# An LSTM with a mixture of experts behind it: which products fill the gaps between the recurrent steps, in which order, and how the last group of steps ends

## The chip, the cores and the metric

The kernel runs on one core of a Trainium2 chip. The metric is the device time of one execution in microseconds; the number given for a kernel is the median of its runs. An execution taken by the hardware profiler gives the trace; its span runs from the program's first to its last instruction.

## The reference

Two sequences (N = 2) of 1024 steps with 256 features go through an LSTM with 256 hidden units. Then every token goes through a router over eight experts, of which the two best count, and through two shared experts. Both layers add to their input.

```python
def step(carry, xw_t):
    prev_h, prev_c = carry
    a = xw_t + prev_h @ Wh
    i, f, o = sigmoid(a[:, :256]), sigmoid(a[:, 256:512]), sigmoid(a[:, 512:768])
    g = tanh(a[:, 768:])
    next_c = f * prev_c + i * g
    next_h = o * tanh(next_c)
    return (next_h, next_c), next_h
x = x + hs                                  # hs: all next_h
shared = sum_e (silu(x @ s_w1[e].T) * (x @ s_w3[e].T)) @ s_w2[e].T / 2
gates = top-2 of sigmoid([x, cond] @ W_router.T), normalized
routed = sum_e gates[:, e] * (gelu(x @ r_w1[e].T) @ r_w2[e].T)
x = x + (shared + routed) / 4
```

The code above is shortened: the reference writes the gates, the sums and the reshapes out. All is float32.

## The kernel before, in words

One Python loop over `t` (L728) writes out all 1024 LSTM steps; each step needs the h of the step before, so the steps run one after the other. A step has these parts:

- **The recurrent block** (L746 to L756): 32 products of h with parts of `wh_sb`, each on 32 weight columns of the array. The four quarters `q` of the output lie on four groups of 32 partitions. In the profile every product is two passes[...], so the block is 64 MATMUL records.
- **The gap**: what TensorE is given between this block and the next one (L757 to L779). It is described below.
- **The cell**: VectorE transposes the gates in PSUM (L787), ScalarE takes sigmoid and tanh (L790, L791), VectorE and ScalarE compute the cell and its tanh (L794 to L807), and VectorE writes the new h (L810) in two halves. The next recurrent block waits for it.

Everything else is spread over the steps by a small planner, the class `Fill`. Four queues hold closures with a cost each: for TensorE (`pe`), for ScalarE, and two for VectorE. The router and experts of a finished group of tokens are put into these queues by `experts` (L286); the products of the LSTM's inputs with Wx (`queue_inputs`, L631) go into the same TensorE queue. `GROUPS` (L36) says how many steps make a group, `PACES` (L38) by how many steps later its products shall be issued, and `run_pe` (L117) takes in each step so many products from the queue that it empties in time, within a cost of `ROOM` = 4 and as long as one of two PSUM banks is free for those that open one. All products go through one helper, so the profile shows them at L255; they are told apart by their tiles: `ps<-wh_sb,h` is the recurrent block, `ps_f<-...` are products of experts, router and LSTM inputs, `ps<-ident,inputs` puts the LSTM's input terms into the PSUM bank where the gates of eight later steps are summed ("input product" from here on), and `ps<-ident` is a product of the identity with itself whose result nobody reads ("idle product").

The gates of eight steps share one pair of PSUM tiles (`TH` = 8). So at each eighth step (an opening, `t % TH == 0`) the tiles change, and during eight steps the eight input products for the next tiles are issued, mostly one in a step. In the gap of a step the order before is: expert products (L758), or, if there were none in this step and none at the opening, an idle product of 256 columns (L761 to L765), and then the input products (L767 to L779).

How many input products a step gets also depends on a count of TensorE's instructions: `fill.issued` counts 4 for a product, and `WAITS` lists the steps in which the program has a further instruction that only waits. Instructions are fetched in blocks of `FETCH` = 256. The loop at L772 chooses the smallest number of input products that keeps the next block's border out of the next `EARLY` = 16 instructions; if none does, the last input product is cut into pieces (`pieces` of `inject`, L654) so that the border falls within them.

Behind the loop, the last group (32 steps, 64 tokens) is issued without steps between (`drain`, L851). What is left of the group before it stands ahead of it in the queue. `last_add` (L532) adds an expert's result to the sum `acc`; 64 tokens lie on two halves of the partitions, with four experts on each. After the last expert a product with `fold` adds the two halves, ScalarE copies the result, and one DMA stores it.

Of the kernel before, what the change touches and what calls it, by code (L numbers as in the profile page):

```python
# [9 lines left out]
F32 = mybir.dt.float32  # L10
# [11 lines left out]
Q = 4  # L22
# [10 lines left out]
TOP_K = 2  # L33
LAST = 32

GROUPS = [128] * 3 + [32] + [128] * 4 + [64, LAST]  # L36

PACES = [128] * 7 + [56, 31, 0]  # L38
FILL_BANKS = 2


# [5 lines left out]


FETCH = 256
EARLY = 16  # L50
WAITS = (
    1, 8, 16, 24, 32, 40, 48, 56, 64, 72, 80, 88, 96, 104, 112, 120, 128, 136, 144, 149,
    152, 157, 160, 160, 165, 168, 176, 181, 184, 189, 192, 197, 200, 208, 216, 224, 232,
    240, 248, 256, 264, 272, 280, 288, 296, 304, 312, 320, 328, 336, 344, 352, 360, 368,
    376, 384, 392, 400, 408, 416, 419, 421, 423, 424, 428, 430, 432, 435, 437, 439, 440,
    440, 447, 448, 456, 464, 472, 480, 488, 496, 504, 512, 520, 528, 529, 536, 544, 552,
    560, 568, 576, 584, 592, 600, 608, 616, 624, 632, 640, 648, 656, 664, 672, 680, 688,
    688, 696, 704, 712, 720, 728, 736, 744, 752, 760, 768, 776, 784, 792, 800, 808, 816,
    824, 832, 840, 848, 856, 864, 872, 880, 888, 896, 904, 912, 920, 928, 930, 933, 935,
    936, 940, 942, 944, 947, 949, 951, 952, 956, 958, 960, 963, 965, 968, 976, 984, 992,  # L60
    999, 1000, 1004, 1006, 1008, 1011, 1013,
)
ISSUED = -188
OUT_SCALE = 1.0 / (NS + TOP_K)
# [9 lines left out]
class Fill:  # L74
# [36 lines left out]
    def run(self, queue, budget):  # L111
        while queue and queue[0][0] <= self.step and queue[0][1] <= budget:
            _, cost, fn = queue.popleft()
            budget -= cost
            fn()

    def run_pe(self, count, room):  # L117
        done = 0
# [16 lines left out]
def lstm_moe_kernel(  # L135
# [117 lines left out]
    def product(*operands, **how):  # L253
        fill.issued += 4
        nc.tensor.matmul(*operands, **how)  # L255
# [30 lines left out]
    def experts(t0, S):  # L286
# [215 lines left out]
        def last_shared_down(c):  # L502
            if c < 0:
                st["down"] = bank()
                x_kqj = st["down"][:W, 0, :].rearrange("p (q k j) -> p k q j", q=Q, k=K)
                for k in range(K):
                    product(
                        x_kqj[:, k], mov[k], ident_s,
                        start=(k == 0), stop=False, skip_group_check=True,
                    )  # L510
                return
            ps, n = st["down"], NS * HS // P
            for g in range(2):
                product(
                    ps[g * W : (g + 1) * W, 0, :], st["h_s"][:, c + g, :W], w2_sb[:, c + g, :],
                    start=(c + g == 1), stop=(c + 2 == n), skip_group_check=True,
                )
            if c + 2 == n:
                fill.to_dve(0.45, lambda: begin_sum(0, ps), lag=0)
# [11 lines left out]

        def last_add(e2, ps):  # L532
            acc = st["acc", 0]
            nc.vector.scalar_tensor_tensor(  # L534
                acc, ps[:, 0, :], st["gates"][:, e2 : e2 + 1], acc, ALU.mult, ALU.add
            )
            fill.let_go()
            if e2 == E // 2 - 1:
                both = bank()[:W, 0, :]
                product(both, fold, acc, start=True, stop=True)  # L540
                total = work.tile([P, D], F32, name="y")[:W]
                nc.scalar.activation(total, both, AF.Copy)  # L542
                nc.sync.dma_start(out=out_tn[t0 : t0 + S], in_=total)

        ups = [
            (int(j == 0), W // P if W > P else 1, lambda b=b, j=j: up(b, j))
# [181 lines left out]
    for t in range(T):  # L728
        fill.step = t
        grp, u = divmod(t, TB)  # L730
        if t % TH == 0:
            cur, nxt = nxt, [gates_tile(m) for m in range(K)]
            ps, turned, busy = [a[0] for a in cur], [a[1] for a in cur], nxt[0][2]
            spare = False
        if u == 0:
            sgm, gf = nxt_results
        if t == 1:
            queue_inputs(0, ROWS)
        if t == XB // 2:
            queue_inputs(1)  # L740
            due = XB
        if t == T - 1:
            residual(grp, int(t - TB in ends), TB)


        for k, m, pair in BLOCKS:  # L746
            for q in range(Q):
                w0 = q * D + m * P + pair * 64
                product(
                    ps[m][q * ROWS : (q + 1) * ROWS],  # L750
                    h_window(t, k, pair),
                    wh_sb[:, k, w0 : w0 + 64],
                    start=False,
                    stop=(t % TH == TH - 1 and k == K - 1 and pair == 1),
                    skip_group_check=True,
                )  # L756
        left = max(1, due - t)  # L757
        done = fill.run_pe(-(-len(fill.pe) // left), ROOM)  # L758
        if t % TH == 0:
            spare = not done  # L760
        if spare and not done:  # L761
            product(
                busy, ident, ident.unsqueeze(1).to_broadcast([P, 2, P]),
                start=(t % TH == 0), stop=False, skip_group_check=True,
            )  # L765

        if t // TH + 1 < T // TH:  # L767
            put = put if t % TH else 0
            fill.issued += WAITS.count(t)

            left = K * Q - put
            count = next(  # L772
                (n for n in range(max(0, t % TH + 1 - put), left + 1)
                 if -(fill.issued + 4 * n) % FETCH > EARLY), left)
            first = -(fill.issued + 4 * count) % FETCH
            for i in range(count):
                more = i == count - 1 and first <= EARLY
                inject(nxt, t // TH + 1, put, 2 + first // 4 if more else 1)
                put += 1  # L779

        rows = slice(N * (t % TH), N * (t % TH + 1))
        gates = [turned[m].rearrange("p (a r) -> p a r", r=PAIR)[:, :, rows] for m in range(K)]
        c_new = [cells[m][:, t % 2] for m in range(K)]
        seen = [stepp.tile([P, N], F32, name=f"seen{m}") for m in range(K)]

        def transpose(m):
            nc.vector.transpose(turned[m], ps[m])  # L787

        def squash(m):
            nc.scalar.activation(sgm[:, u, m, :, :, 1], gates[m][:, 0:3], AF.Sigmoid)  # L790
            nc.scalar.activation(gf[:, u, m, :, 0], gates[m][:, 3], AF.Tanh)  # L791

        def forget(m):
            nc.vector.tensor_mul(gf[:, u, m, :, 1], sgm[:, u, m, 2, :, 1], c_prev[m][:, :, 1])  # L794

        def cell(m):

            nc.vector.tensor_copy(seen[m], gf[:, u, m, :, 0])  # L798
            nc.vector.tensor_tensor_scan(  # L799
                c_new[m].rearrange("p n z -> p (n z)"),  # L800
                sgm[:, u, m, 0].rearrange("p n z -> p (n z)"),
                gf[:, u, m].rearrange("p n z -> p (n z)"),
                0.0, ALU.mult, ALU.add,
            )

        def squash_cell(m):
            nc.scalar.activation(cells[m][:, 2, :, 0], c_new[m][:, :, 1], AF.Tanh)  # L807

        def output(m):
            nc.vector.tensor_mul(h_cols(t + 1)[:, m], sgm[:, u, m, 1, :, 1], cells[m][:, 2, :, 0])  # L810

        for fn in (transpose, squash):
            for m in range(K):
                fn(m)
        for m in range(K):
            forget(m)
            cell(m)
            squash_cell(m)
        for m in range(K):
            output(m)  # L820
        if u == TB // 2 and t + TB < T:
            nxt_results = results()
        else:
            fill.run(fill.act, 1.0)
        c_prev = c_new
        if rest and t % LOAD == 0:
            load_next()
        if t == 2 * TB:
            lg = bank()[:, 0, :E]
            fill.banks -= 1  # L830
            fill.pe.extend((0, 1, lambda k=k: condition_scores(lg, k)) for k in range(K))
        if (t + 1) % XB == 0 and t + 1 + XB < T:
            queue_inputs((t + 1) // XB + 1)
        if u < TB - 1:
            fill.run_dve(0.6)
            continue
        if t < T - 1:
            residual(grp, int(grp == 0 or t - TB in ends), TB)
        if t in ends:
            residual(grp + 1, 0, 1)  # L840
            if t == T - 1:
                drain(fill)
                fill.last = True
                fill.banks += 4
            t0, S, pace = ends[t]
            experts(t0, S)
            due = t + pace
# [80 lines left out]
```

## Time and profile before

| what | value |
|---|---|
| median of three runs | 2257.78 us (2252.64 to 2258.61) |
| profiled execution, its own time | 2256.97 us |
| its span | 2254.8 us |
| mean granted TensorE clock | 0.996 |
| TensorE busy | 2033.5 us |
| VectorE busy | 1571.3 us |
| ScalarE busy | 909.5 us |
| time between the ends of the recurrent chain: first and last write of h (L810, second half) | 11.6 and 2233.9 us |
| last store issued (L543) | 2251.8 us |

The profile gives each instruction's start and length. An engine's busy time counts its own instructions; the idle time before an instruction is put down to the instruction whose semaphore ended it. A group's mean mixes shapes unless it says so. "PEclk" and the clock in the view by windows are the share of its full clock that TensorE was granted.

### The profile page before, as it was taken

The page shows a single profiled execution, that of the slowest core. Times are in us where ns is not written, and L with a number is a line of the kernel's source. Part 1 is how long each engine was busy: PE and PEld are TensorE (multiplying, and loading weights), DVE is VectorE, ACT ScalarE, POOL GpSimd, SP SyncE. Part 2 cuts the span into 40 slices and gives each one's busy share as a digit, 9 for nine tenths or more (in the row PEclk, how much of TensorE's full clock was granted, in tenths as well). Part 3 has the DMA queues.
Part 4 walks back from the last instruction along what each step waited for, and adds up shares of the span by engine and source line. Part 5 has one row for each costly group of instructions (what it writes and reads, how often), then busy time and mean ns, then how long its engine had stood idle before and what let it go on. Part 6 is the DMA issues. An engine that isn't in the chain of part 4 may idle for free.

```text
span 2254.8 us, 159246 instructions
## 1 busy us (share of the span) xinstructions
PE 2033.5 (90%) x70612; PEld 1484.8 (66%) x70612; DVE 1571.3 (70%) x11041; ACT 909.5 (40%) x6487; POOL 2.7 (0%) x9
## 2 busy tenths in 40 slices
PE   8988899888989889998798899988898988989998
PEld 6666666666666666777666666666666666667787
DVE  5666667776777667777667767676676776667776
ACT  3334344433444334443344443444434344334443
POOL 0000000000000000000000000000000000000000
PEclk9999999999999999999999999999999999999999
DMA  2111100000000000000000000000000000000000
GB/s 65 35 35 35 35 28 5 5 5 7 7 5 5 5 7 7 5 7 7 5 6 5 5 5 7 7 4 5 5 7 7 4 5 5 7 7 5 5 9 7
DMA packets 15330, 23.84 MB, mean 11 GB/s; under 512 B 2864, under 2 KB 14128, under 8 KB 14640
## 3 DMA queue, kind: packets, MB, share of 16 engines
q1 hardware_dynamic: 14352, 12.62, 1.9%
q8 instruction: 552, 9.04, 1.7%
q14 instruction: 138, 1.13, 0.2%
q10 hardware_dynamic: 288, 1.05, 0.1%
HBM read 11.56 MB, written 2.10 MB: 6 GB/s over the span
## 4 chain that ended last, share of the span: by engine, by line
PE 61%; DVE 36%; issue 3%; DMA 0%; SPq 0%; ACT 0%
PE ps L255 53%; DVE ps L787 10%; DVE c L799 10%; PE ps_f L255 8%; DVE results L794 7%; DVE seen L798 6%; DVE h L810 3%; DMA wh_sb<-in_wh_dram 0%; SPq L165 0%; DVE acc L534 0%; SPq L173 0%; SPq L171 0%; SPq L170 0%; DVE acc L492 0%; ACT y L542 0%
## 5 line engine op out<-in xcount | busy, mean ns | idle before, releaser
L255 PE MATMUL ps<-wh_sb,h 128*32 128x64 f32 x65536 | 1143.8, 221 | 214.3 <-DVE h L810 210.5
L255 PEld LDWEIGHTS ps<-wh_sb,h 128*32 128x32 f32 x65536 | 975.1, 110 | 393.1 <-DVE h L810 386.8
L787 DVE STREAM_TRANSPOSE ps<-ps 128x64 f32<-128x64 f32 x2048 | 543.4, 265 | 498.5 <-PE ps L255 426.0
L790 ACT ACTIVATE results<-ps 128x6 f32<-128x6 f32 x2048 | 361.3, 176 | 1103.8 <-DVE ps L787 1009.4
L810 DVE TENSOR_TENSOR h<-results,c 128x2 f32<-128x2 f32 x2048 | 314.2, 153 | 168.4 <-ACT c L807 168.2
L807 ACT ACTIVATE c<-c 128x2 f32<-128x2 f32 x2048 | 321.5, 157 | 217.5 <-DVE c L799 181.7
L799 DVE TENSOR_TENSOR_SCAN c<-results 128x4 f32<-128x4 f32 x2048 | 358.2, 175 | 0.0
L791 ACT ACTIVATE results<-ps 128x2 f32<-128x2 f32 x2048 | 342.4, 167 | 0.0
L798 DVE COPY seen<-results 128x2 f32<-128x2 f32 x2048 | 332.8, 162 | 0.0
L794 DVE TENSOR_TENSOR results<-results,c 128x2 f32<-128x2 f32 x2048 | 319.3, 156 | 0.0
L255 PEld LDWEIGHTS ps<-ident,inputs 128*32 128x32 f32 x2090 | 124.0, 108 | 265.7 <-issue 228.4
L255 PE MATMUL ps<-ident,inputs 128*32 128x64 f32 (+2 forms) x2090 | 263.9, 230 | 0.3
L255 PE MATMUL ps_f<-x2T,w_sb 128*128 128x256 f32 (+3 forms) x640 | 173.4, 379 | 0.0
L255 PE MATMUL ps_f<-x2T,r_sb 128*128 128x256 f32 (+3 forms) x640 | 173.2, 378 | 0.0
L255 PE MATMUL ps_f<-r_sb,h_r 128*128 128x256 f32 (+1 forms) x520 | 165.9, 419 | 0.9 <-DVE acc L492 0.9
L255 PEld LDWEIGHTS ps_f<-x2T,r_sb 128*128 128x128 f32 (+1 forms) x640 | 88.5, 184 | 22.8
L255 PEld LDWEIGHTS ps_f<-x2T,w_sb 128*128 128x128 f32 (+1 forms) x640 | 86.7, 184 | 21.8 <-issue 0.2
L255 PEld LDWEIGHTS ps_f<-r_sb,h_r 128*128 128x128 f32 (+1 forms) x520 | 80.0, 184 | 23.3 <-DVE acc L492 1.3
L255 PE MATMUL ps_f<-xT_sb,wx_sb 128*128 128x256 f32 (+2 forms) x384 | 84.5, 346 | 0.3 <-ACT inputs L613 0.3
L255 PE MATMUL ps<-ident 128*128 128x256 f32 x232 | 82.8, 443 | 1.4 <-POOL ident masks.py:199 1.4
L255 PE MATMUL ps_f<-w_sb,h_s 128*128 128x256 f32 (+1 forms) x256 | 82.6, 419 | 0.0
L492 DVE SCALAR_TENSOR_TENSOR acc<-ps_f,gate,acc 128x256 f32<-128x256 f32 (+1 forms) x128 | 61.1, 478 | 1.2 <-PE ps_f L255 1.0
(87 smaller groups left out, 475.1 us busy)
## 6 DMA issues: line engine op xcount, KB each, us to landing
r_sb<-in_r_w1T_dram SPq DMA_DIRECT2D x16, 128.0 KB, 2.5
r_sb<-in_r_w2T_dram SPq DMA_DIRECT2D x16, 128.0 KB, 2.1
out_dram<-acc SPq DMA_DIRECT2D x15, 128.0 KB, 2.1
xT_sb<-in_xT_dram SPq DMA_DIRECT2D x14, 128.0 KB, 2.5
wx_sb<-in_wx_dram ACTq DMA_DIRECT2D x2, 512.0 KB, 4.3
wh_sb<-in_wh_dram SPq DMA_DIRECT2D x2, 512.0 KB, 6.2
w_sb<-in_s_w1T_dram SPq DMA_DIRECT2D x8, 128.0 KB, 2.2
w_sb<-in_s_w3T_dram SPq DMA_DIRECT2D x8, 128.0 KB, 2.2
```

The costliest lines, as they stand in the source:

```text
L255: nc.tensor.matmul(*operands, **how)
L492: nc.vector.scalar_tensor_tensor(acc, ps, st["gate"][:, i, e : e + 1], acc, ALU.mult, ALU.add)
L787: nc.vector.transpose(turned[m], ps[m])
L790: nc.scalar.activation(sgm[:, u, m, :, :, 1], gates[m][:, 0:3], AF.Sigmoid)
L791: nc.scalar.activation(gf[:, u, m, :, 0], gates[m][:, 3], AF.Tanh)
L794: nc.vector.tensor_mul(gf[:, u, m, :, 1], sgm[:, u, m, 2, :, 1], c_prev[m][:, :, 1])
L798: nc.vector.tensor_copy(seen[m], gf[:, u, m, :, 0])
L799: nc.vector.tensor_tensor_scan(c_new[m].rearrange("p n z -> p (n z)"), sgm[:, u, m, 0].rearrange("p n z -> p (n z)"), gf[:, u, m].rearrang ...
L807: nc.scalar.activation(cells[m][:, 2, :, 0], c_new[m][:, :, 1], AF.Tanh)
L810: nc.vector.tensor_mul(h_cols(t + 1)[:, m], sgm[:, u, m, 1, :, 1], cells[m][:, 2, :, 0])
```

## The change

- **A wide product in each step.** Where a step has no expert product, an idle product of 256 columns is issued, whatever the opening had. For that, each opening must start the idle product's PSUM area: with 256 columns if the opening has no expert product, else with a product of 32 columns (`wide`), which stands first in the gap, with the wait for the PSUM tile's last reader.
- **Order in the gap.** A new method `ready_pe` counts, without issuing, how many expert products the step will take. Then the input products are issued, then the expert products, then an idle product if there was none of them and the step is no opening. At an opening the idle product comes first. The count of input products now looks for a border that is over `EARLY` = 12 instructions (20 in the last 32 steps) behind the end of the gap and not among its last two.
- **Groups.** The groups and paces at the end change, so that the group before the last is fully issued within the loop.
- **The last shared product** writes its two parts (`k`) on two halves of the partitions.
- **The last sum** is made in two halves of 128 columns: an addition, a product with `fold`, a copy and a DMA for each.

`WAITS` is rewritten for the new order (left out here).

```diff
-GROUPS = [128] * 3 + [32] + [128] * 4 + [64, LAST]
+GROUPS = [128] * 3 + [32] + [128] * 3 + [64] * 3 + [LAST]
-PACES = [128] * 7 + [56, 31, 0]
+PACES = [128] * 6 + [60, 60, 48, 27, 0]
-EARLY = 16
+EARLY = 12
...
+    def ready_pe(self, count, room):
+        done, banks = 0, self.banks
+        for opens, cost, _ in self.pe:
+            if done == count or opens > banks or cost > room:
+                break
+            banks -= opens
+            room -= cost
+            done += 1
+        return done
...
     def last_shared_down(c):
-                x_kqj = st["down"][:W, 0, :].rearrange("p (q k j) -> p k q j", q=Q, k=K)
+                x_kqj = st["down"][:, 0, :].rearrange("p (q k j) -> p k q j", q=Q, k=K)
                 for k in range(K):
                     product(
-                        x_kqj[:, k], mov[k], ident_s,
-                        start=(k == 0), stop=False, skip_group_check=True,
+                        x_kqj[k * W : (k + 1) * W, k], mov[k], ident_s,
+                        start=True, stop=False, skip_group_check=True,
                     )
...
     def last_add(e2, ps):
+            if e2 < E // 2 - 1:
+                cols = [slice(0, D)]
+            else:
+                cols = [slice(0, P), slice(P, D)]
+                total = work.tile([P, D], F32, name="y")[:W]
+            for i, c in enumerate(cols):
+                nc.vector.scalar_tensor_tensor(
+                    acc[:, c], ps[:, 0, c], st["gates"][:, e2 : e2 + 1], acc[:, c],
+                    ALU.mult, ALU.add,
+                )
+                if len(cols) > 1:
+                    both = bank()[:W, 0, :P]
+                    product(both, fold, acc[:, c], start=True, stop=True)
+                    nc.scalar.activation(total[:, c], both, AF.Copy)
+                    nc.sync.dma_start(out=out_tn[t0 : t0 + S][:, :, c], in_=total[:, c])
...
-        done = fill.run_pe(-(-len(fill.pe) // left), ROOM)
-        if t % TH == 0:
-            spare = not done
-        if spare and not done:
+        count = -(-len(fill.pe) // left)
+        done = fill.ready_pe(count, ROOM)
+        opens = t % TH == 0
+        if opens:
+            wide = busy[:, :1, :ROWS] if done else busy
             product(
-                busy, ident, ident.unsqueeze(1).to_broadcast([P, 2, P]),
-                start=(t % TH == 0), stop=False, skip_group_check=True,
-            )
+                wide, ident, ident[:, : wide.shape[2]].unsqueeze(1).to_broadcast(wide.shape),
+                start=True, stop=False, skip_group_check=True,
+            )
+            put = 0
+        then = 4 * (done or not opens) + WAITS.count(t)
+        early = EARLY + (8 if t >= T - LAST else 0)
         if t // TH + 1 < T // TH:
...
+            ways = range(max(0, t % TH + 1 - put), K * Q - put + 1)
+            first = [-(fill.issued + 4 * n + then) % FETCH for n in ways]
+            n = next((n for n, f in zip(ways, first) if early < f < FETCH - 2), ways[-1])
+            for i in range(n):
+                more = i == n - 1 and not early < first[-1] < FETCH - 2 and n == ways[-1]
+                inject(nxt, t // TH + 1, put, 2 + min(first[-1], early) // 4 if more else 1)
                 put += 1
+        fill.issued += WAITS.count(t)
+        fill.run_pe(count, ROOM)
+        if not (done or opens):
+            product(
+                busy, ident, ident.unsqueeze(1).to_broadcast(busy.shape),
+                start=False, stop=False, skip_group_check=True,
+            )
```

## The prediction

> **What bounds the kernel now.** I read the page first.
>
> ```profile
> span 2254.8 us, 159246 instructions
> ...
> PE 2033.5 (90%) x70612; PEld 1484.8 (66%) x70612; DVE 1571.3 (70%) x11041; ACT 909.5 (40%) x6487; POOL 2.7 (0%) x9
> ...
> PE 61%; DVE 36%; issue 3%; DMA 0%; SPq 0%; ACT 0%
> ```
>
> The chain of waits is TensorE and VectorE in turn: one serial loop of 1024 LSTM steps. No engine's busy share matters, only the length of a step. I took the period of all steps from the second L810 row of each: the median is 2.154 us, and 1023 periods sum to 2222.3. So 1023 x 2.154 = 2203.5 cannot move, and 18.7 us is excess that sits in single steps. Ahead of the loop lie 11.6 us (to the first h), behind the last h 20.9.
>
> The TensorE timeline (start, duration, engine, line, operation; in brackets the idle time before it and its releaser) shows what can lengthen a step: the gap between two recurrent blocks (64 passes on 32 weight columns; every product has two passes).
>
> ```profile
> 1017.37 1.13 PE L255 MATMUL ps_f<-r_sb,h_r 128*128 128x256 f32 x4
> 1018.49 1.10 PE L255 MATMUL ps<-wh_sb,h 128*32 128x64 f32 x64
> 1019.52 1.13 PE L255 MATMUL ps_f<-r_sb,h_r 128*128 128x256 f32 x4
> 1020.59 0.24 PE L255 MATMUL ps<-ident,inputs 128*32 128x64 f32 x1
> ```
>
> ```profile
> 1468.94 0.61 PE L255 MATMUL ps_f<-wr_sb,x2T 128*128 128x8 f32 x4
> 1469.49 0.30 PE L255 MATMUL ps<-ident,inputs 128*32 128x64 f32 x2
> ```
>
> Two expert products of 256 columns fill the gap: they begin 0.149 us behind the last recurrent pass, and the next 32-column pass begins 1.07 us after they did. The single records give these constants (medians over all steps): 32-column work to 128-column work 0.149; first to second pass of a 256-column product 0.320, every further pass 0.216; last 256-column pass to the next 32-column pass 0.309 (0.205 for 64 columns, 0.186 for 8); two passes of an input product 0.080 apart behind a 128-column product, but 0.049 + 0.056 = 0.105 where it comes straight behind the recurrent block. From the last recurrent pass to the next block, which waits for h, are 1.272 us. Two expert products need 0.149 + 0.320 + 0.432 + 0.309 = 1.210, so 0.06 is spare; one needs 0.778.
>
> Summing these constants over each gap of the built program (in its own order) gives 5.3 us of excess for the kernel before; its steps, without those of the next two causes, measure 5.2.
>
> Second cause, the clock, from the view by windows (the column after the busy times is the granted clock):
>
> ```profile
> 40.10:50.30 10.20, 8.07 (x252) 6.77 (x245) 4.26 (x34) 2.37 (x18) 0.00 (x0) 0.50 0.08 20
> ...
> 1470.30:1473.60 3.30, 3.30 (x100) 3.11 (x92) 1.39 (x11) 0.79 (x6) 0.00 (x0) 0.50 0.02 5
> 1750.20:1753.50 3.30, 3.30 (x82) 2.48 (x85) 1.59 (x12) 0.79 (x6) 0.00 (x0) 0.50 0.00 0
> ```
>
> The first hits steps 13 to 16, whose gaps are nearly empty (3.26 us over the median), the others the steps of router products of 8 columns (1.08 and 1.14). Together 5.5.
>
> Third cause, instruction fetch.
>
> ```profile
> q8 instruction: 552, 9.04, 1.7%
> ```
>
> ```profile
> 471.89 1.37 PE L255 MATMUL ps<-wh_sb,h 128*32 128x64 f32 x64 [0.42 <-DVE h L810]
> ```
>
> The program has 141,399 TensorE instructions, 256 for each of the 552 packets. Where a multiple of 256 falls on the last four products of a recurrent block, it often takes longer, as the 1.37 here against 1.10; elsewhere there is no cost. By position (28, 29, 30, 31 of 32) I count 27, 16, 46 and 2 such places, costing 0.02, 0.04, 0.13 and 0.4 us in the mean: about 8.0. 5.2 + 5.5 + 8.0 is the 18.7.
>
> **The change, part by part.**
>
> Input products ahead of the experts'. For one input product and two expert products the gap now needs 0.105 + 1.210 = 1.315, which is 0.043 over 1.272. Before it cost 0.024 to 0.037 in such steps. With the further steps of three or more products, gaps other than the openings below go from 5.3 to 7.3: +2.0. Gaps with one expert product stay under 1.272: nothing.
>
> A wide product in each step. Steps without an expert product get 256 columns, 0.778 + 0.105: hidden by the wait for h, which has 0.39 to spare. But each eighth step that has expert products gets a product of 32 columns first, then the input product, then the experts'. That is two more changes between 32 and 128 weight columns. No row has 32 columns. By the 8-column row the narrow product costs 0.133 + 0.186, by the 64-column row 0.160 + 0.205; I take 0.320, since 32 columns stream within the weight load (0.19) that bounds the 8-column row. It cannot be below nothing: it stands in program order ahead of the rest. Gap: 0.149 + 0.320 + 0.080 + 0.149 = 0.698, then one expert product 0.629 makes 1.327 (+0.055), two make 1.759 (+0.487). The built program has 18 such openings with two 256-column products (8.7 us, one without an input product), 68 with one (4.1), 20 with other mixes (2.8): +15.6. What is queued behind the narrow product's wait on ScalarE are these experts' products and the recurrent block; the same wait of 18 openings before was over at once (0.154 to the first pass). The same sum over a gap of four router products and one of 256 columns at step 928 gave 0.508 against 0.514 measured, so a full gap does push h out one for one.
>
> Here the Trainium skill weighs in. "TensorEngine Tiling (Array Packing)", Key Properties, says that changing the tiling mode drains TensorE. By columns alone 32 of 256 would cost an eighth of an expert product, 0.03 to 0.05; 106 of them could then add at most some 5 us; by the drains in the rows it is 15.6. I take the rows.
>
> The clock. The Trainium skill's "TensorE: Matmul & The Clock Gate" (Why this matters for your kernels) asks only for no idle gap over about 3 us between bursts. By that rule the wide product buys nothing: no gap before is over 1.4 us. The rows say otherwise (clock 0.50 at 40.1), so I take the first lapse away, -3.3; by the rule the sum would end 3.3 higher. The router pairs keep their 8-column products and get no wide one. Six groups of 128 steps make such pairs possible, two fell before; I expect about one, -1.3 (bounds -2.2 and +3).
>
> Fetch. The rebuilt order has 24, 25 and 17 places at 28, 29 and 30, none at 31. At 0.02, 0.08 (gaps with one product stalled 0.16 to 0.19) and 0.13 that is 4.8 against 7.6 (step 1's 0.36 stays): -2.8, bounds -3.8 and +1.
>
> No product behind the loop.
>
> ```profile
> 2232.64 1.13 PE L255 MATMUL ps_f<-r_sb,h_r 128*128 128x256 f32 x4
> 2234.68 1.99 PE L255 MATMUL ps_f<-r_sb,h_r 128*128 128x256 f32 x8 [0.91 <-DVE acc L492]
> 2236.60 0.41 PE L255 MATMUL ps<-wr_sb,x2T 128*64 128x8 f32 x8
> ```
>
> The 8 passes at 2234.68 waited for a bank that an addition (L492) frees, and the last group's router products wait behind them. They are gone. The router products then wait for the last residual (L674, ends 2234.22), the following products for the bank, free at 2234.66: they start at 2234.72 instead of 2236.85. TensorE paces the tail, so -2.1. Of five additions (0.48 each), three remain, and VectorE's later chain moves up by as much. The smaller groups at the end cost more products in the loop (1056 against 992 expert ones); their gaps are in the sums above.
>
> Last sum in two halves. Two additions of 128 columns instead of 0.48, then half a product, half a copy, and a second DMA issue (SP takes 0.55 for one). The second half is ready about 0.1 sooner, but SP is still busy with the first: 0, bounds -0.3 and +0.3. Spreading the last shared product over row halves is off the path.
>
> Sum: +2.0 + 15.6 - 3.3 - 1.3 - 2.8 - 2.1 = +8.1. Against the profiled execution's own 2256.97 (span 2254.8 and 2.2 around it) that is 2265; its time is 0.8 under the median, so 2265 to 2266 for that. I say 2265.
>
> **Rivals.**
>
> 1. The narrow product is covered: TensorE loads the experts' weights while the input product still runs, so no second change is paid. For it: weight loads overlap passes within one kind of work (66% busy beside 90%). Against: every one of 769 input products behind a 256-column product began 0.308 us or more behind its last pass. Then the 15.6 go: -7.5, 2249.5, faster. It decides wherever the openings with two expert products exceed the median by under 0.1 us.
> 2. Fetch lands worse: places inside a gap stall products that have no slack, and the early places at 29 stall as those at 30 do. +4 on the forecast: 2269.
> 3. The clock still lapses, at the router pairs and at the start, so the wide product does not do what it is for: +5, 2270.
>
> **How the numbers follow.** 0.3% (6.8 us) is about what a measurement tells from no change. The forecast case, 2265, has 0.66, rival 1 0.12, rivals 2 and 3 0.11 each. The bounds of its terms (fetch -1 to +3.8, clock -1 to +4, narrow product 0 to +4) and the 6 us between the three runs make about +-6 around 2265, and the limit of slower, 2264.6, cuts it nearly in the middle: of the 0.66, 0.34 is slower and 0.32 within. Rivals 2 and 3 give 0.19 slower, 0.03 within; rival 1 0.07 faster, 0.05 within. Faster 0.07, same 0.40, slower 0.53. The range, 2255 to 2272, leaves out most of rival 1 and little else.
>
> **What would show it.** Right: openings with two expert products some 0.49 above 2.154, with one 0.05; gaps with two and one input product 0.04; no clock of 0.50 near 40 us; router products at about 0.4 us behind the last h; a tail near 18.8 us. Wrong: openings at the median; or long recurrent blocks as often as before.

## The result, and the profile after

The changed kernel takes 2271.44 us in the median of four runs (2269.27 to 2274.03), the kernel before in runs beside it 2256.79 (four runs). The ratio is 1.0068, its 95% interval 1.005 to 1.0086: slower by 14.6 us, where I forecast 8. The profiled execution takes 2271.10 us against 2256.97, its span is 14.4 us longer. Of all the executions below one, of run b2, took 3206 us at a mean granted clock of 0.818; it is in no ratio.

First the page after: span, engine times, the chain by engine, the instruction fetch.

```profile
span 2269.2 us, 160208 instructions
...
PE 2005.7 (88%) x71078; PEld 1518.8 (67%) x71078; DVE 1572.6 (69%) x11067; ACT 911.7 (40%) x6489; POOL 2.7 (0%) x9
...
q8 instruction: 556, 9.11, 1.7%
...
PE 67%; DVE 30%; issue 3%; ACT 0%; POOLq 0%; POOL 0%
```

TensorE has more instructions but less busy time, and still its share of the chain rises from 61% to 67%: in more steps the gap, not the cell on VectorE, decides when the next block starts. The median step is 2.155 us (before 2.154), so all of the loss but at most 1 us (1023 x 0.001) sits in single steps again.

The view by windows at the place where the clock was 0.50 before; the column after the busy times is the granted clock, now 1.00:

```profile
40.10:50.30 10.20, 8.89 (x332) 6.41 (x334) 6.42 (x51) 3.72 (x28) 0.00 (x0) 1.00 0.15 43
```

The TensorE timeline of an opening with two expert products of 256 columns (step 440; start, duration, operation):

```profile
970.25 1.10 PE L266 MATMUL ps<-wh_sb,h 128*32 128x64 f32 x64
971.28 0.41 PE L266 MATMUL ps<-ident 128*128 128x32 f32 x2
971.62 0.30 PE L266 MATMUL ps<-ident,inputs 128*32 128x64 f32 x2
971.85 1.13 PE L266 MATMUL ps_f<-x2T,r_sb 128*128 128x256 f32 x4
972.91 1.10 PE L266 MATMUL ps<-wh_sb,h 128*32 128x64 f32 x64
```

From block to block are 2.66 us. The narrow product holds TensorE 0.34 us, the input product 0.23 more, and only then do the experts' products begin. The tail, from the last product of the group before:

```profile
2249.24 1.13 PE L266 MATMUL ps_f<-r_sb,h_r 128*128 128x256 f32 x4
2250.97 0.41 PE L266 MATMUL ps<-wr_sb,x2T 128*64 128x8 f32 x8 [0.61 <-DVE x2T L691]
2251.27 2.09 PE L266 MATMUL ps_f<-x2T,w_sb 128*64 128x64 f32 x64
```

The router products wait only for the last residual and start 0.50 us behind the last h (2250.47); from there to the end are 18.70 us, before 20.94.

### The profile page after: what moved, and what is told of

The parts are those of the page before. It is cut to its first block, busy times and chain, and to the rows that moved or that the text cites. A ratio compares the mean times of both kernels' runs of the same rounds, so it can differ in the third digit from the quotient of the medians.

```text
span 2269.2 us, 160208 instructions
## 1 busy us (share of the span) xinstructions
PE 2005.7 (88%) x71078; PEld 1518.8 (67%) x71078; DVE 1572.6 (69%) x11067; ACT 911.7 (40%) x6489; POOL 2.7 (0%) x9
## 4 chain that ended last, share of the span: by engine, by line
PE 67%; DVE 30%; issue 3%; ACT 0%; POOLq 0%; POOL 0%
PE ps L266 55%; PE ps_f L266 12%; DVE ps L811 9%; DVE c L823 8%; DVE results L818 6%; DVE seen L822 5%; DVE h L834 2%; ACT inputs L630 0%; DVE acc L551 0%; POOLq L947 0%; ACT y L558 0%; DVE x2T L691 0%; ACT c L831 0%; POOL ident masks.py:197 0%; POOLq masks.py:199 0%
## 5 line engine op out<-in xcount | busy, mean ns | idle before, releaser
L266 PEld LDWEIGHTS ps<-wh_sb,h 128*32 128x32 f32 x65536 | 964.4, 110 | 602.2 <-DVE h L834 595.8
L266 PE MATMUL ps<-wh_sb,h 128*32 128x64 f32 x65536 | 1131.5, 221 | 247.9 <-DVE h L834 245.8
L266 PE MATMUL ps<-ident,inputs 128*32 128x64 f32 (+4 forms) x2154 | 258.9, 219 | 8.0 <-issue 7.2
L266 PEld LDWEIGHTS ps<-ident,inputs 128*32 128x32 f32 x2154 | 151.7, 110 | 21.8 <-issue 16.5
L266 PE MATMUL ps<-ident 128*128 128x256 f32 (+1 forms) x504 | 146.5, 375 | 1.4 <-POOL ident masks.py:199 1.4
L266 PEld LDWEIGHTS ps_f<-x2T,r_sb 128*128 128x128 f32 (+1 forms) x704 | 95.7, 184 | 23.8 <-issue 1.6
L266 PEld LDWEIGHTS ps_f<-x2T,w_sb 128*128 128x128 f32 (+1 forms) x704 | 94.1, 184 | 23.3 <-issue 1.7
L266 PEld LDWEIGHTS ps<-ident 128*128 128x128 f32 x504 | 76.6, 190 | 24.6 <-POOL ident masks.py:199 1.4
```

## The experiments

The runs came in five sets, each with runs of the kernel before beside it; its medians lie between 2249.4 and 2256.8 us. So I compare ratios within a set, and sums within a profile. `WAITS` is rewritten for each program with a changed order; the cuts below leave that out. Three sums of a profile are used: **gaps** (the constants of the prediction, added over each gap, plus what steps without fetch and clock show besides), **clock** (steps in a lapse), **fetch** (the excess of all steps that hold a place where a new block of 256 instructions begins). In the pair above, gaps went from 5.4 to 23.8, clock from 5.5 to 1.2, fetch from 7.8 to 10.6.

**Second profiles of both kernels.** No edit.

> The kernel before, unchanged, for a second profile beside the next three on one chip. If the three causes of its excess belong to the program: again 5 us in full gaps, 5 to 6 from lapses of the clock near 40 us and at the router products, and 5 to 8 at recurrent products 28 to 31, with nothing at the 70 places inside gaps. If the fetch or the clock differ by chip, those two terms move and the gaps by constants stay.

> The changed kernel, unchanged, for a second profile on the same chip as the kernel before. My theory: openings with two 256-column products 0.50 over the median and with one 0.075 again, 22.9 in gaps by constants; 77 places of the fetch inside gaps with a 128-column product behind cost 4 to 6 us, those on recurrent products 28 to 30 2 to 4 less than before; the tail 2.2 shorter, the clock 3 to 5 less; ratio 1.005 to 1.008. Rival (my prediction's own fetch term was right and the first profile had bad luck): places inside gaps under 1.5 us, ratio 1.0035 to 1.004.

Measured: ratio 1.0066 (1.0053 to 1.0079) for the changed kernel, 0.9998 (0.9989 to 1.0007) for the unchanged one against itself. In this pair gaps are 5.4 and 23.5, clock 0 and 0, fetch 3.9 and 6.2. The gaps belong to the program; clock and fetch differ by execution. The fetch again went up, where I had it go down.

**Without the narrow product** (a1):

```diff
-            wide = busy[:, :1, :ROWS] if done else busy
+        if opens and not done:
             product(
-                wide, ident, ident[:, : wide.shape[2]]...
+                busy, ident, ident...
```

> The changed kernel without the narrow opening product of 32 columns: at a step t%8==0 that has expert products none is issued (an opening without them keeps its 256-column idle product). All else stays, so the order of waits is a little different. My theory, that the narrow product pays for two more changes between 32 and 128 weight columns: the 18 openings with two 256-column products go from about 0.50 over the median step to about 0.04, those with one from 0.076 to nothing; the sum over all gaps of the constants falls from 22.9 to 8.8, so 2271.4 - 14.1 = 2257. Rival 1 of the prediction (the switch is covered, the openings are long for another reason such as the fetch): within 2 us of 2271.

Measured: 1.0002 (0.9992 to 1.0011). Against 1.0066 to 1.0068 for the changed kernel that is 14.4 to 14.8 us, as the theory of the drains has it. Rival 1 is out. The same step 440 without the narrow product, 2.19 us from h to h instead of 2.66:

```profile
962.01 0.27 PE L266 MATMUL ps<-ident,inputs 128*32 128x64 f32 x2
962.21 1.13 PE L266 MATMUL ps_f<-x2T,r_sb 128*128 128x256 f32 x4
963.27 1.10 PE L266 MATMUL ps<-wh_sb,h 128*32 128x64 f32 x64
```

**Experts' products ahead of the input products, narrow product kept** (a2): the new groups and halves in the kernel before, and in its gap

```diff
+        if t % TH == 0 and fill.ready_pe(count, ROOM):
+            wide = busy[:, :1, :ROWS]
+            product(wide, ident, ident[:, :ROWS]..., start=True, stop=False, ...)
         done = fill.run_pe(count, ROOM)
-        if spare and not done:
+        if not done:
             product(busy, ident, ...)
```

> The changed kernel (groups, halves, narrow opening product, idle product in each step without expert products) but with the input products behind the experts' as in the kernel before, and with its rule for places of the fetch. The narrow product then stands straight ahead of the experts' and costs no second change. Theory of the drains: openings with two 256-column products about 0.17 over the median, gaps in sum 10.6 instead of 22.9 (-12.3). Theory of fetch places inside the gap: 7 places with a 128-column product behind them instead of 77 (-5 to -6.6), but 83 places on recurrent products 28 to 31 instead of 66, 39 of them on product 30 (+4). Together about 2257. If places inside the gap cost nothing: 2263. If it is the narrow product itself and not the two changes that costs: 2268.

Measured: 1.0012 (1.0002 to 1.0021), 12 us less than the changed kernel. The same narrow product costs less where no input product stands between it and the experts':

```profile
963.98 0.41 PE L266 MATMUL ps<-ident 128*128 128x32 f32 x2
964.23 1.11 PE L266 MATMUL ps_f<-x2T,r_sb 128*128 128x256 f32 x4
965.27 0.24 PE L266 MATMUL ps<-ident,inputs 128*32 128x64 f32 x1
```

Narrow product to experts' product are 0.25 us here, 0.57 in the changed kernel. Openings with two 256-column products stand 0.29 over the median in a2, 0.50 in the changed kernel. So at such an opening the two further changes of weight columns are 0.21, and more is left to the product by itself than the 0.17 that I had expected. That nearly all of the loss is gone all the same is due to the openings with one expert product: they have room for the product by itself and stand at the median in a2, 0.076 over it in the changed kernel.

**Further input products behind the experts'** (a3):

```diff
-            for i in range(n):
+            for i in range(min(n, 1)):
...
+        for i in range(1, n):
+            inject(...)                  # behind run_pe and the idle product
```

> The changed kernel with only the first input product of a step ahead of the experts' products; where the rule for the fetch asks for further ones, they come behind them. Places of the fetch inside a gap with a 128-column product at or behind them fall from 77 to 33; those on recurrent products 28 to 30 stay 66, the gaps by constants 23.6 instead of 22.9. Theory that a place inside the gap stalls products that have no slack (rival 2 of the prediction): -3 to -6 on 0.7, so 2266 to 2269. If those places cost nothing and the 6.6 us of these steps are the number of input products: 2271 to 2273, with the same steps long.

Measured: 1.0068 (1.0051 to 1.0085), no gain that the times show; the interval is wider than the 3 us in question. The profile's fetch sum is 4.0 (4.9 to 10.6 in the profiles of the changed kernel and a1), one profile where repeats of one program scatter by 2. What it does show is that the idle time that ended with "issue" in front of input products falls to 0.9 us, from 4.1 to 7.2 in five profiles of the changed kernel. By times inconclusive, by the place of the stalls on the side of rival 2.

**The rule steers by wrong places** (s1):

```diff
-ISSUED = -188
+ISSUED = -316
```

> The changed kernel with one constant moved, the count of instructions issued ahead of the loop (-188 to -316), so that its rule steers by places that are 128 instructions off. Products and their order are nearly the same. Places inside a gap with a 128-column product behind: 2 instead of 77; on recurrent products 28, 29, 30, 31: 20, 20, 29, 37 instead of 24, 25, 17, 0. Theory (a place costs by where it falls: 0.07 in such a gap, 0.02, 0.05, 0.13 and 0.4 at 28 to 31): -5 and +17, so about 2283, with long recurrent blocks (1.2 to 1.6 instead of 1.1) at the 37 places on product 31. If only the recurrent places count: 2288. If the place of the fetch is not the cause of long blocks and long gaps: 2271, with the same gaps long as in the changed kernel.

Measured: 1.0109 (1.0094 to 1.0124), 9 to 10 us over the changed kernel's ratio (of which 1.0 is a longer tail, 19.70 us). Fetch is 14.4 in sum, 11.5 of it at products 28 to 31, nothing in the gaps. That the places matter is shown; but product 31 cost 0.11 in the mean, product 30 0.20, which is not the order that I had assumed (0.4 and 0.13).

**Places kept off products 28 to 31** (c0), the kernel before with

```diff
-                 if -(fill.issued + 4 * n) % FETCH > EARLY), left)
+                 if EARLY < -(fill.issued + 4 * n) % FETCH <= 110
+                 or -(fill.issued + 4 * n) % FETCH > 128), ...)
```

> The kernel before with one rule changed: the number of input products of a step is chosen, where that is possible, so that the next fetch place does not fall on products 28 to 31 of the next recurrent block. Places there: 7, 5, 26 and 2 instead of 27, 16, 46 and 2; inside gaps still none with a 128-column product behind. Theory (the place sets the cost): -3.4 at the first profile's prices, 0.9985 of the kernel before. If the position does not matter: 1.000, with as much lost elsewhere.

Measured: 1.0003 (0.9993 to 1.0013), no gain, and a fetch sum of 5.7. The places at 28 to 31 fell from 91 to 40 and cost 2.5, but those ahead of them, which had cost 0.3 to 0.6, now cost 4.0, nearly all of it at 26 and 27. This is one of them (the gap of step 554 and the block of step 555; "issue" means that nothing in the profile held TensorE):

```profile
1209.78 0.31 PE L255 MATMUL ps<-ident,inputs 128*32 128x64 f32 x6
1210.28 0.98 PE L255 MATMUL ps<-wh_sb,h 128*32 128x64 f32 x53 [0.18 <-DVE h L813]
1211.60 0.41 PE L255 MATMUL ps<-wh_sb,h 128*32 128x64 f32 x11 [0.35 <-issue]
```

This felled my theory that the position sets the price. Three input products in the gap instead of none had moved the place from 30 to 27, and the stall went with it. What stayed the same is the time since the place before: about 3.2 us, with one wait for h in it. A window of 256 instructions holds one such wait or two, and lasts about 3.0 to 3.5 or 3.8 to 4.2 us. Sorted by that, the short windows hold nearly all of the fetch sum in the kernels with the experts' products first: 71 to 77 of some 545 windows, 4.2 to 9.1 us of it; all others together within 0.8 us of nothing.

**A longer step, the same places** (s2), s1 with

```diff
-            forget(m)
+            for _ in range(4):
+                forget(m)
```

> The kernel of run s1_shifted with one cheap multiplication of the cell (L818, its result unchanged) issued four times over in each step, so that every step is longer; TensorE's program, its order and every place of the fetch are the same. New theory: a fetch costs something only where the 256 instructions ahead of its place run in under about 3.4 us, which is where only one wait for h lies among them (in s1_shifted 79 such windows with 12.2 us of excess, the 470 others 0.6). With a longer step these windows last 0.3 us or more longer: their excess falls from 12 to under 3 us with the places unmoved. Rival (the place itself decides, products 28 to 31): 8 us or more of excess stay at these 106 places, the largest 0.5 or more.

Measured: 3411 us in one execution, as the step grew to 3.24 us, more than I had meant (one such multiplication takes 0.156 us in the profile). TensorE's order and places are those of s1. Outside lapses of the clock no step exceeds the median by more than 0.005 us. The block of step 592 in s1, and then in s2:

```profile
1303.14 1.09 PE L266 MATMUL ps<-wh_sb,h 128*32 128x64 f32 x62 [0.19 <-DVE h L834]
1304.99 0.30 PE L266 MATMUL ps<-wh_sb,h 128*32 128x64 f32 x2 [0.75 <-issue]
```

```profile
1980.82 1.10 PE L266 MATMUL ps<-wh_sb,h 128*32 128x64 f32 x64 [1.27 <-DVE h L834]
1981.85 0.41 PE L266 MATMUL ps<-ident 128*128 128x32 f32 x2
```

The block that stalled for 0.75 us in front of its last product runs through when the window is longer. The place alone does nothing; the time does.

The trace even has the fetch itself: one 16 KB packet of q8 behind each place. For the stalled block of s1, the DMA view of 1301.2 to 1305.2 us in 40 slices of 0.1 (the packet is entered at 1302.5; 1.4% of 16 engines' 4 us is 0.9 us):

```profile
DMA  0000000000000500000000000000000000000000
...
q8 instruction: 1, 0.02, 1.4%
```

By the records it starts at 1302.56, 1.3 us behind the place before it, and ends at 1303.48, 0.8 us ahead of the time at which the block, with its usual 1.10 us, would have ended. (The time of a place is counted here at the end of the product that stands at it.) In the median a packet starts 0.6 us behind the place before (0.4 to 1.1 for eight in ten) and takes 0.9 to 1.6 us. With the lead, the time from a packet's end to the moment at which its place is due by the step's usual course, the places of 17 profiles (all but s2) sort like this:

```
lead of the packet       places in recurrent blocks        places in gaps
                         number  mean excess  over 0.1     number  mean excess  over 0.1
under 1.5 us                181     0.333        88%          204     0.137        47%
1.5 to 1.7                  217     0.097        43%          146     0.019        10%
1.7 to 1.9                  347     0.008         3%          172    -0.004         2%
over 1.9                   7320     0.000         0%          701    -0.010         0%
```

For 131 stalls of over 0.25 us in recurrent blocks, lead and stall together are 1.76 us in the median, 1.57 to 1.91 in nine of ten: where TensorE is held at a place, the product there ends about 1.76 us after the packet has landed. It starts some 0.25 us earlier: in the block above at 1304.99, 1.51 us after the packet's end. In s2 no lead is under 1.7.

**The rest of the change, part by part.** b1 is the kernel before with the new groups, paces, halves and the last shared product; b2 has only

```diff
-            spare = not done
-        if spare and not done:
+            spare, put = not done, 0
+        if (spare or put >= Q) and not done:
```

and b3 both. c1 is b3 with the rule of c0.

> The kernel before with the new groups, paces, the last sum in halves and the last shared product over row halves, and nothing else. By my sum: the tail behind the last h 18.7 instead of 20.9 (-2.2), full gaps 5.8 instead of 5.3 (+0.5), fetch and clock as before: 0.9993 of the kernel before (0.999 to 1.000). Rival (the groups' products make other steps late, a wait takes the gain): tail as above and the ratio over 1.0005.

> The kernel before with the idle product of 256 columns in nearly each step without expert products (only not where a group of eight has opened with expert products and its first four input products are not yet in), and no narrow product. Theory: no lapse of the clock near 40 us, mean clock of its runs 0.999 instead of 0.998, and some -1.5 us: 0.9993. Rival (lapses come from the router products, not from empty gaps): clock 0.998 and 1.000.

> The kernel before with the new groups and halves and the idle product of run b2_idle_each together, input products behind the experts', the old rule for the fetch, no narrow product. If the parts add: -2.2 (tail) +0.4 (gaps) -1.5 (clock) = -3.3, 0.9985 of the kernel before, its 95% interval under 1. If the new rule of run c1_best was worth something, this is slower than that one (0.9993); by the theory of windows that rule was worth nothing and its further input products cost 1 to 2 us, so this is faster.

> The kernel before with the parts of the change that the sum books as gains, and none of its costs: the new groups (tail -2.2, gaps +0.6), the last sum in halves (0), a 256-column idle product in steps without expert products but no narrow product at an opening (one clock lapse less, -3.3), input products behind the experts', and the rule of the run above for the fetch (places 10, 7, 35 and 0 at products 28 to 31: -2). Together -6 to -7: 0.997 of the kernel before, faster than both. Rival (the gains are not independent: the tail's or the clock's gain comes only with the costs): 1.000 or more.

Measured: b1 0.9997 (0.9985 to 1.0008), b2 0.9998 (0.9989 to 1.0007), b3 0.9995 (0.9986 to 1.0004), c1 0.9993 (0.9985 to 1.0002). The tail is 18.71 us in b1, b3 and c1, as expected. b2's profile has no lapse in the loop, and eleven of its twelve runs have a mean clock of 0.9998 (without the one of 3206 us), against 0.9982 in the 29 runs of the kernel before and 0.9974 in the twelve of b1 beside them: its theory of the clock held. But gains of 2 us each are within these intervals, so no version is shown to be faster than the kernel before, and the expectation for c1 (0.997) was too high: its rule gained nothing, as in c0. b3 is not shown to differ from c1.

**More profiles with input products ahead.** No edit against the changed kernel and a1.

> The changed kernel, unchanged, third profile. If input products ahead make the fetch dearer: fetch in sum 7.5 to 9 us in the mean of this and the next two (against 5.7 for the order before). If it does not move: 4.5 to 6.5. In both cases gaps by constants 23 to 24, clock mean 0.999 to 1.000, ratio 1.005 to 1.0075.

> The changed kernel, unchanged, fourth profile: as after_3. The same steps long at openings (0.50 and 0.075 over the median); the long steps of the fetch partly other ones than in the first two profiles, if single fetches differ by execution.

> The changed kernel, unchanged, fifth profile: as after_3 and after_4; the mean of the five then has an error of about 1 us.

> The changed kernel without the narrow product, second profile, as an eighth one with input products ahead: fetch 4.9 us in its first; with a dearer fetch 7 or more, without 4 to 6.5; ratio 0.999 to 1.001.

Measured: ratios 1.0076, 1.0075, 1.0075 (1.0046 to 1.0105 together) and 0.9994 (0.998 to 1.0008). Fetch: 5.5, 8.8, 8.3, and 9.8 for a1. The changed kernel's five profiles have 7.9 in the mean (deviation 2.1), the eight with the experts' products first 6.2 (1.8). The difference, +1.7, has an error of 1.1. With a1's two profiles (4.9 and 9.8) and a3's added, the eight with input products ahead have 7.3, and the difference is 1.1 with an error of about 1. The three new profiles have 7.5 in the mean, at the edge of what I had expected if input products ahead make the fetch dearer. With this scatter that is not shown, but a fall of 2.8 is excluded.

## Why the prediction was wrong

The forecast was +8.1 against its profiled execution, and the pair of profiles gave +14.1. The terms:

| term | predicted | first pair | second pair |
|---|---|---|---|
| gaps: openings and the others | +17.6 | +18.3 | +18.0 |
| clock | -4.6 | -4.3 | 0 |
| fetch | -2.8 | +2.8 | +2.4 |
| behind the last h | -2.1 | -2.2 | -2.2 |
| ahead of the first h, and around the span | 0 | -0.5 | -0.6 |

**Right, and tested: the narrow product.** Openings with two expert products of 256 columns stand 0.502 over the median (0.487 forecast), those with one 0.076 (0.055), gaps with two and an input product 0.037 (0.043). a1 takes all of it away. The sum by columns alone, some 5 us, was rightly set aside.

**Right: the tail.** Its -2.2 stands in the profile, and b1 has it alone. The halves did a little that I had put at nothing: between the span and the execution's own time lie 2.2 us in 84 runs of the kernel before, and 1.8 to 2.1 in the mean of each kernel with the halves.

**The step that failed: fetch.** "At 0.02, 0.08 [...] and 0.13 that is 4.8 against 7.6 [...]: -2.8, bounds -3.8 and +1." (The prices as printed give 4.7.) In its place the two pairs have +2.8 and +2.4, and all profiles together +1.7. The term counted only places in recurrent blocks and priced them by position. For these places its size was about right: stalls with a lead under 1.7 us in blocks cost 6.1 us in the mean of the eight profiles with the experts' products first and 2.8 in the five of the changed kernel, -3.3. That was luck in part, as c0 shows that the position does not set the price. What I left out are the places inside gaps, because 70 of them had cost nothing in the trace of before. They were free for a reason that the change removes. A place behind the experts' products, late in the gap, comes 3.8 us after the one before it in the median. With input products ahead of the experts', and the further ones of the rule there too, the place comes early in the gap, after 3.2 us; the lead falls under 1.7 us at 40 to 48 places of a profile instead of 2 to 4. They cost 2.7 to 5.7 us, 3.9 in the mean. (2.8 and 3.9 leave 1.2 of the 7.9 at places with longer leads, which this does not explain.) The stalls stand on the page, as idle time in front of input products. Before, and then after:

```profile
L255 PE MATMUL ps<-ident,inputs 128*32 128x64 f32 (+2 forms) x2090 | 263.9, 230 | 0.3
```

```profile
L266 PE MATMUL ps<-ident,inputs 128*32 128x64 f32 (+4 forms) x2154 | 258.9, 219 | 8.0 <-issue 7.2
```

How the loss in these gaps divides between gaps and fetch rests on the constants alone. Each step with more than one input product holds a place, before and after, so none shows the products without a fetch. These steps, 62 to 69 in a profile, stand 0.9 us over the median in sum in both profiles of before, and 6.5 to 9.0 in three of the changed kernel.

The clearest stall (step 564):

```profile
1241.71 1.10 PE L266 MATMUL ps<-wh_sb,h 128*32 128x64 f32 x64 [0.31 <-DVE h L834]
1242.63 0.29 PE L266 MATMUL ps<-ident,inputs 128*32 128x64 f32 x8
1243.37 0.42 PE L266 MATMUL ps<-ident,inputs 128*32 128x13 f32 x8 [0.46 <-issue]
1243.72 0.70 PE L266 MATMUL ps_f<-x2T,w_sb 128*128 128x256 f32 x2
1244.35 1.10 PE L266 MATMUL ps<-wh_sb,h 128*32 128x64 f32 x64
```

The place lies in the fifth of eight input products. TensorE stands for 0.46 us, then still has the rest, a product of 256 columns and a change of columns to do, and the next block starts 0.5 us late. Had the experts' product been ahead of the place, most of the stall would, by the constants (0.39 to spare with one such product), have fallen into the wait for h. That is the first half of rival 2, to which I gave 0.11. Its other half, that places at 29 stall as those at 30 do, did not come: 0.03 in the mean at 24 or 25 places in both profiles.

Here the trace of before would have sufficed: it holds the 552 packets with their times, and its 41 leads under 1.7 us in blocks carry all of its fetch sum. I took a rule by position from them where the cause was a duration. The Trainium skill, "Runtime: NRT & Kernel Launch" (Instruction fetch mechanics), says that crossing a boundary of 16 KB costs one tail bump, "mostly hidden". By that the term is near nothing before and after; the profiles have 3.9 to 14.4 us of it, so the rows decide.

**Right in direction, too large: the clock.** No profile with the wide idle product has the lapse at 40 us, but of the four without it only the first one has it (the second of the kernel before, c0 and b1 have none there). So it is not shown that the product removes this lapse; that it raises the mean clock is shown by b2, apart from its one execution of 3206 us. Lapses elsewhere stay: 3.4 us at a clock of 0.50 begin at 874.5 us in the first profile of the changed kernel, at 1106.1 and 1481.6 in its third. I took -4.6 from one execution with a mean clock of 0.996. In 84 runs of the kernel before it is 0.998 in the mean, from 0.995 to 1.000, and each 0.001 goes with 1.3 us of span; 15 runs of the changed kernel have 0.9992. So the usual gain is some 1.5 us (0.0011 at 1.3 us for each 0.001), and rival 3 is a part of the miss.

With these, gaps +18.2, clock -1.5, fetch +1.7, tail -2.2 and the end -0.3 make +15.9, where the medians of three sets differ by 13.3 to 14.7, and the ratios, 1.0066 to 1.0076, make it 14.9 to 17.1. Open stay how much of the fetch's +1.7 is real within its error of 1.1, and what makes some packets start 1 to 2 us behind their place instead of 0.6.

## What to carry over

A cost that the trace shows at a position may be the cost of a time: before it is used for a changed order, sort the same records by the time since the event before and see which of the two splits them better. A place where something was free is a place with slack, and a change that moves work ahead of it takes the slack away. A term that comes from an event of chance (a lapse of the clock, a late packet) is taken from all runs, not from the one that was profiled.

## What the hardware showed that I had not expected

- TensorE's instructions come in packets of 16 KB, one behind each place. Where TensorE had to wait, the product at the place ended 1.76 us after the packet's end in the median; with the packet's start (0.6 us) and its own 0.9 to 1.6 us that is 3.3 to 4 us from place to place. TensorE waits where it runs 256 instructions sooner, up to 1.0 us at one place (s1).
- One program loses different amounts from one execution to the next: the kernel before 5.5 and 0 us to lapses of the clock in the loop, the changed kernel 5.5 to 8.8 us to the fetch in three executions of one set.
- In s2, where the waits for h are 1.1 us longer, 332 us of the execution ran at a granted clock of 0.50. No profile of a kernel with the usual step has more than 20 us of that. But the long wait is not the only way there: the execution of b2 with a mean clock of 0.818 had the usual step. It has no profile, and its cause stays open.
- In s2, multiplications of 128 x 2 elements on VectorE that write the same tile, one behind the other, start 0.18 to 0.19 us apart, each 0.156 us long in the profile: six more in a step made it 1.08 us longer. The copy behind them starts before the last one has ended.
